# Head-output matmuls and product matmuls in opposite column halves of TensorE, in turns

## The chip, the cores and the metric

The kernel runs on one core of a Trainium2 chip. The metric is the time of one execution on the device in microseconds (us); the median over several runs is given. TensorE multiplies, VectorE (DVE), ScalarE (ACT) and GpSimd (POOL) do the rest, and SyncE (SP) issues most transfers.

## The reference

The input x is 128 batches of 128 rows of 768 numbers, adj 128 matrices of 128 x 128; all is f32. The layer is a pre-norm attention with a mask and a bias from adj, 12 heads of 64.

```python
h = jnp.maximum(_layernorm(x, axis=-1), 0.0)
q = _split_heads(h @ Wq + bq)           # also k and v
scores = jnp.einsum('bhqd,bhkd->bhqk', q, k) / jnp.sqrt(HD)
scores = scores + beta * adj[:, None]
scores = jnp.where(adj[:, None] > 0, scores, -9e15)
probs = jax.nn.softmax(scores, axis=-1)
out = jnp.einsum('bhqk,bhkd->bhqd', probs, v)
return x + out.transpose(0, 2, 1, 3).reshape(B, N, D)
```

## The kernel before

The batches go through in 32 groups of four (G is 0 to 31), so that a group has 512 rows. For each group three slices of the projections are computed: "qk0" (queries and keys of heads 0 to 5), "v" (all values) and "qk1" (queries and keys of heads 6 to 11). Each slice is a 2 x 3 by 3 x 3 block product done with 15 block products in place of 18, on sums of blocks; only the first slice of group 0 is done plainly (L575). The function `slice_of` runs the 15 products in order. `product` (L385) does one: for each of two halves i of its output and each of two halves c of the contraction, it issues two matmuls (L401), one into the lower 64 output partitions (q = 0) and one into the upper 64 (q = 64). Output partitions 0 to 63 and 64 to 127 belong to the two column halves of TensorE, so each matmul uses 64 of its 128 columns. Both matmuls of a pair read the same moving operand of 256 columns, with different weights. Each f32 matmul stands in the trace as two records (two passes), each with its own load of 64 weight columns.

A product adds into a PSUM bank of its chain (a, b, c or d, the third entry of `PRODUCTS`); after the product, DVE (L427 for q and k, L418 and L413 for v) or ACT (L423) reads the bank out, and the next product of the same chain adds on. Eight PSUM banks are handed out in the order in which they were given back (`take`, `give`).

The attention of a group is laid into the slices that follow. `scores` (L437) does the score matmuls (L448) for three pairs of heads at once behind product 1 of a slice, adds the mask and bias on DVE (L452), and takes exponentials on ACT (L455), which gives the tiles e. Behind products 5, 8 and 11 `attend` (L474) puts one generator into the queue `between`. The generator, `attend_steps` (L477), does the head outputs of one pair of heads (i = 0, 1) for the four batches of the group (r and g, two each): in each step one matmul of 65 columns into each column half (L486; 64 columns of v and one of ones that sums the weights). Every turn of the queue, `turn` (L380), runs one step: 

```python
    def turn():
        while between and next(between[0], None) is None:
            between.popleft()
```

`product` calls `turn` four times, behind each pair of its matmuls. An attend has eight steps, so it lies over two products. When the four head outputs of one r are in a bank, `weigh` (L457) divides them by their sums on DVE (L460, L461, L463, L467; in group 0 the division is on ACT, L470), and the bank is given back. At the end GpSimd adds the result to x (L495) and SP stores it (L496). The last group uses other functions for its last heads (`scores_half`, `attend_half`), which the change leaves as they are.

Of the kernel before, what the change touches and what calls it, by code (L numbers as in the profile page):

```python
# [17 lines left out]
P = 128  # L18
# [103 lines left out]
def direct(ctx, tc, x, adj, wq, bq, wk, bk, wv, bv, beta, out, bad):  # L122
# [12 lines left out]
    HD = D // HEADS  # L135
# [244 lines left out]
# [5 lines that stand above are left out]
    def product(G, sl, n, order):  # L385

        an, bn, chain, uses = PRODUCTS[n]
        mine = [i for i in order if PRODUCTS[i][2] == chain]
        first = n == mine[0]
        if first:  # L390
            banks[chain] = take()
        p = banks[chain].rearrange("p (i w) -> p i w", i=2)
        a, b = A[G, an], wt[sl, bn]
        for i in range(2):
            for c in range(2):
                if sl == "v":
                    lhs, rhs = a[:, c, i * N:(i + 1) * N], b[:, c, :]
                else:
                    lhs, rhs = b[:, c, i * P:(i + 1) * P], a[:, c, :]
                for q in range(0, P, HD):  # L400
                    nc.tensor.matmul(p[q:q + HD, i, :], lhs[:, q:q + HD], rhs, start=(first and i == 0 and c == 0),  # L401
                                     stop=(c == 1), skip_group_check=True)
                turn()
        for (r, j), sign in uses:
            key = (G, sl, r, j)
            if sl == "v":
                got = p.rearrange("p g (h d) -> p (g h) d", d=HD)
                if key not in vt:
                    vt[key] = vring[nv[0] % len(vring)]
                    nv[0] += 1  # L410
                    o4 = vt[key].rearrange("p (g h) e -> p g h e", g=2)[:, :, :, 0:HD]
                    bias = bv_b[:, j * 2 * P:(j + 1) * 2 * P].rearrange("p (h d) -> p h d", d=HD)
                    added[G] = nc.vector.tensor_tensor(o4, bias[:, None, :, :].to_broadcast([P, 2, 4, HD]),  # L413
                                                        p.rearrange("p g (h d) -> p g h d", d=HD),
                                                        ALU.add if sign > 0 else ALU.subtract)
                else:
                    o = vt[key][:, :, 0:HD]
                    added[G] = nc.vector.tensor_tensor(o, o, got, ALU.add if sign > 0 else ALU.subtract)  # L418
            elif key not in qk:
                t = qk[key] = work.tile([P, 2, H2], F32, tag="qk", name=f"{sl}_{G}_{r}_{j}", bufs=8)  # L420
                oc = j + 3 * int(sl[2])
                for i in range(2):
                    opened[0] = nc.scalar.activation(t[:, i, :], p[:, i, :], AF.Identity, bias=bqk[:, i, oc:oc + 1],  # L423
                                                     scale=float(sign))
            else:
                t = qk[key]
                added[G] = nc.vector.tensor_tensor(t, t, p, ALU.add if sign > 0 else ALU.subtract)  # L427
        if n == mine[-1]:
            give(banks.pop(chain))
# [27 lines left out]
    def weigh(G, oc, r, pa, o):  # L457

        t = stat.tile([P, 2, 4], F32, tag="sm", name=f"sm_{G}_{oc}_{r}")
        nc.vector.tensor_scalar(t[:, 0], pa[:, :, HD], TINY, None, op0=ALU.max)  # L460
        nc.vector.reciprocal(t[:, 1], t[:, 0])  # L461
        s = seen[:, 8 * r:8 * r + 8]
        nc.vector.tensor_tensor(s, s, t.rearrange("p i b -> p (i b)"), ALU.max)  # L463

        def divide():
            if G:
                nc.vector.tensor_mul(o, pa[:, :, 0:HD], t[:, 1, :, None].to_broadcast([P, 4, HD]))  # L467
            else:
                for b in range(4):
                    nc.scalar.activation(o[:, b], pa[:, b, 0:HD], AF.Copy, scale=t[:, 1, b:b + 1])  # L470

        return divide

    def attend(G, oc):  # L474
        between.append(attend_steps(G, oc))

    def attend_steps(G, oc):  # L477
        o = work.tile([P, 2, 4, HD], F32, tag="o", name=f"o_{G}_{oc}", bufs=2)
        for r in range(2):
            bank = take()  # L480
            pa = bank[:, 0:4 * VE].rearrange("p (b e) -> p b e", e=VE)
            for g in range(2):
                for i in range(2):
                    h = 2 * oc + i
                    for q in range(0, P, HD):
                        nc.tensor.matmul(pa[q:q + HD, 2 * g + i, :], es[G, oc, i][:, 2 * r + g, q:q + HD],  # L486
                                         vt[G, "v", r, h // 4][:, 4 * g + h % 4, :], start=True, stop=True,
                                         skip_group_check=True)
                    if g == i == 1:
                        weigh(G, oc, r, pa, o[:, r])()  # L490
                        give(bank)
                    if r + g + i < 3:
                        yield True
        t = xo[G, oc]
        nc.gpsimd.tensor_add(t, t, o.rearrange("p a (b j) d -> p (a b) (j d)", j=2))  # L495
        nc.sync.dma_start(out[G * GRP:(G + 1) * GRP, :, oc * P:(oc + 1) * P].rearrange("g n d -> n g d"), t)  # L496
        yield True
# [58 lines left out]
    def slice_of(G, sl, todo, order=range(len(PRODUCTS))):  # L556
        for at, n in enumerate(order):
            product(G, sl, n, order)
            for f in todo.get(at, ()):
                f()  # L560
# [372 lines left out]
```

## Time and profile before

| what | value |
|---|---|
| median of 4 runs (lowest to highest) | 2882.28 us (2881.76 to 2882.48) |
| the profiled execution | 2882.06 us |
| its span, first to last instruction | 2880.2 us |
| granted TensorE clock | 0.999 of full |
| busy PE / weight loads / DVE / ACT / POOL | 100% / 70% / 69% / 28% / 12% |
| L401 matmul records | 22800, 256 columns |
| L486 matmul records | 6048, 65 columns |
| L448 matmul records | 6048, 128 columns |

The page of the profile has the busy time of each engine, the granted clock by slices of the span, the chain of work that ended last (followed back from the last instruction), and groups of instructions by line, with busy time, mean duration of one, and the idle time of the engine before them. PE is TensorE's matmuls, PEld its weight loads. The durations of matmul records are modelled and overlap; times from start to start tell what one costs.

### The profile page before, as it was taken

How to read it: one execution, taken by the hardware profiler on the slowest of the kernel's cores; microseconds unless marked ns; L12 is line 12 of the kernel's file. 1: busy time of each engine (PE TensorE's matmuls, PEld its weight loads, DVE VectorE, ACT ScalarE, POOL GpSimd, SP SyncE). 2: the span in 40 equal slices, each digit the busy share in tenths (PEclk: the TensorE clock that was granted, in tenths of full speed). 3: DMA queues.
4: the chain of work that ended last, by engine and by line, in shares of the span. 5: the costliest groups of instructions: out<-in, count | busy, mean ns of one | idle time of the engine just before them, and what ended most of it. 6: DMA issues, size and time to landing. Idle time of an engine off the chain costs nothing.

```text
span 2880.2 us, 81474 instructions
## 1 busy us (share of the span) xinstructions
PE 2871.2 (100%) x35330; PEld 2010.6 (70%) x35330; DVE 1974.2 (69%) x4503; ACT 814.1 (28%) x1750; POOL 334.8 (12%) x320
## 2 busy tenths in 40 slices
PE   9999999999999999999999999999999999999999
PEld 7766667666676666766667766677666676666766
DVE  7867666676666676766766667667676676766665
ACT  2522222232331323313232232322222222323221
POOL 3111011110111110110101101011010111101100
PEclk9999999999999999999999999999999999999999
DMA  9222223222232222332222322223222232222311
GB/s 203 77 61 77 64 79 84 80 68 65 78 88 82 67 70 68 88 87 63 77 70 81 86 66 78 64 82 84 69 79 63 79 84 79 69 69 73 88 38 42
DMA packets 418907, 220.93 MB, mean 77 GB/s; under 512 B 110704, under 2 KB 418160, under 8 KB 418544
## 3 DMA queue, kind: packets, MB, share of 16 engines
q1 hardware_dynamic: 412864, 213.45, 27.2%
q8 instruction: 277, 4.54, 0.7%
q0 software_dynamic: 3808, 1.84, 0.5%
q10 hardware_dynamic: 1872, 0.40, 0.1%
q14 instruction: 86, 0.70, 0.1%
HBM read 164.76 MB, written 50.33 MB: 75 GB/s over the span
## 4 chain that ended last, share of the span: by engine, by line
PE 99%; DVE 0%; DMA 0%; issue 0%; SPq 0%; DVEq 0%
PE bank L401 86%; PE bank L448 6%; PE bank L486 6%; PE bank L575 1%; DMA x<-in_x_dram 0%; PE bank L511 0%; PE bank L529 0%; PE bank L626 0%; DVE o L467 0%; DVE strow L607 0%; DVE e L515 0%; SPq L169 0%; PE bank L278 0%; DVE rows L621 0%; DVE xo L538 0%
## 5 line engine op out<-in xcount | busy, mean ns | idle before, releaser
L401 PE MATMUL bank<-S,qk_T 128*64 128x256 f32 x7056 | 867.5, 380 | 0.0
L427 DVE TENSOR_TENSOR qk<-qk,bank 128x512 f32<-128x512 f32 x630 | 425.5, 676 | 394.3 <-PE bank L401 391.0
L423 ACT ACTIVATE qk<-bank,bqk 128x256 f32<-128x256 f32 x756 | 316.5, 470 | 1133.8 <-PE bank L401 947.1
L486 PEld LDWEIGHTS bank<-v,e 128*64 128x64 f32 x6048 | 433.2, 137 | 220.4
L401 PEld LDWEIGHTS bank<-S,qk_T 128*64 128x64 f32 x7056 | 454.7, 137 | 173.3 <-ACT e L455 5.0
L401 PE MATMUL bank<-S,qk_B 128*64 128x256 f32 x4032 | 543.4, 380 | 0.0
L495 POOL TENSOR_TENSOR xo<-xo,o 128x512 f32<-128x512 f32 x189 | 252.5, 1336 | 2258.6 <-DVE o L467 1587.3
L401 PE MATMUL bank<-A,qk_T 128*64 128x256 f32 x4032 | 490.1, 379 | 0.0
L486 PE MATMUL bank<-v,e 128*64 128x65 f32 x6048 | 430.8, 221 | 0.0
L401 PE MATMUL bank<-v_T,S 128*64 128x256 f32 x3584 | 421.8, 380 | 0.0
L455 ACT ACTIVATE e<-e 128x512 f32<-128x512 f32 x378 | 227.7, 629 | 655.3 <-DVE e L452 654.8
L418 DVE TENSOR_TENSOR v<-v,bank 128x512 f32<-128x512 f32 x320 | 220.0, 687 | 232.4 <-PE bank L401 230.6
L401 PEld LDWEIGHTS bank<-v_T,S 128*64 128x64 f32 x3584 | 254.8, 137 | 130.4 <-issue 5.7
L401 PEld LDWEIGHTS bank<-A,qk_T 128*64 128x64 f32 x4032 | 262.8, 137 | 100.8 <-issue 0.2
L452 DVE SCALAR_TENSOR_TENSOR e<-bank,biasT 128x512 f32<-128x512 f32 x378 | 231.9, 683 | 85.4 <-PE bank L448 85.4
L401 PEld LDWEIGHTS bank<-S,qk_B 128*64 128x64 f32 x4032 | 236.3, 138 | 55.6 <-issue 0.2
L401 PE MATMUL bank<-v_B,S 128*64 128x256 f32 x2048 | 243.2, 379 | 0.0
L401 PE MATMUL bank<-v_T,A 128*64 128x256 f32 x2048 | 237.9, 379 | 0.0
L331 ACT ACTIVATE x<-x,block 128x192 f32<-128x192 f32 x464 | 217.6, 536 | 65.7 <-DMA block<-row 63.7
L338 DVE STREAM_TRANSPOSE A<-x 128x256 f32<-128x256 f32 x378 | 213.2, 612 | 4.0 <-ACT x L331 4.0
L401 PEld LDWEIGHTS bank<-v_B,S 128*64 128x64 f32 x2048 | 147.3, 137 | 73.8
L401 PEld LDWEIGHTS bank<-v_T,A 128*64 128x64 f32 x2048 | 147.1, 137 | 73.9
(93 smaller groups left out, 1668.8 us busy)
## 6 DMA issues: line engine op xcount, KB each, us to landing
x<-in_x_dram SPq DMA_DIRECT2D x504, 96.0 KB, 2.7
xo<-in_x_dram SPq DMA_DIRECT2D x189, 256.0 KB, 3.1
out_dram<-xo SPq DMA_DIRECT2D x189, 256.0 KB, 2.4
half<-in_x_dram SPq DMA_DIRECT2D x232, 192.0 KB, 2.5
adj<-in_adj_dram SPq DMA_DIRECT2D x128, 64.0 KB, 2.7
block<-row SPq DMA_DIRECT2D x464, 1.0 KB, 1.7
qk_T<-in_L_gnn_Wq_dram SPq DMA_DIRECT2D x13, 128.0 KB, 4.1
qk_T<-in_L_gnn_Wk_dram SPq DMA_DIRECT2D x13, 128.0 KB, 3.8
```

The costliest lines, as they stand in the source:

```text
L331: nc.scalar.activation(t, t, AF.Relu, bias=shift[G, n], scale=rstd[G, n])
L338: last = nc.vector.transpose(t[:, :, g * N:(g + 1) * N].rearrange("p c (b i) -> p c b i", i=SQ), src)
L401: nc.tensor.matmul(p[q:q + HD, i, :], lhs[:, q:q + HD], rhs, start=(first and i == 0 and c == 0), stop=(c == 1), skip_group_check=True)
L418: added[G] = nc.vector.tensor_tensor(o, o, got, ALU.add if sign > 0 else ALU.subtract)
L423: opened[0] = nc.scalar.activation(t[:, i, :], p[:, i, :], AF.Identity, bias=bqk[:, i, oc:oc + 1], scale=float(sign))
L427: added[G] = nc.vector.tensor_tensor(t, t, p, ALU.add if sign > 0 else ALU.subtract)
L448: nc.tensor.matmul(ps[oc, i][k:k + HD, g * N:(g + 1) * N], t[r, 1, at][:, k:k + HD], t[r, 0, at], start=True, stop=True)
L452: taken[0] = nc.vector.scalar_tensor_tensor(e, ps[oc, i].rearrange("p (g n) -> p g n", g=GRP), SCORE_CAP * ISCALE, biasT[G], op0=ALU.min, ...
L455: nc.scalar.activation(e, e, AF.Exp, scale=1.0 / ISCALE)
L486: nc.tensor.matmul(pa[q:q + HD, 2 * g + i, :], es[G, oc, i][:, 2 * r + g, q:q + HD], vt[G, "v", r, h // 4][:, 4 * g + h % 4, :], start=Tru ...
L495: nc.gpsimd.tensor_add(t, t, o.rearrange("p a (b j) d -> p (a b) (j d)", j=2))
L575: last = nc.tensor.matmul(p[:, i, at], b[:, c, i * P:(i + 1) * P], a[:, c, at], start=(k == 0 and i == 0 and c == 0), stop=(c == 1), skip_ ...
```

## The change

A step of `attend_steps` becomes two matmuls into the same column half (heads i = 0 and 1), first the upper half (q = 64), then the lower. `turn` is called behind each single matmul of a product and no longer behind a pair: behind the product's matmul into the lower half comes a step into the upper half, and the other way round. A product has eight turns now, and an attend, still of eight steps, lies in one product.

```diff
@@ product
                 for q in range(0, P, HD):
                     nc.tensor.matmul(p[q:q + HD, i, :], lhs[:, q:q + HD], rhs, start=(first and i == 0 and c == 0),
                                      stop=(c == 1), skip_group_check=True)
-                turn()
+                    turn()
@@ attend_steps
             for g in range(2):
-                for i in range(2):
-                    h = 2 * oc + i
-                    for q in range(0, P, HD):
+                for q in (HD, 0):
+                    for i in range(2):
+                        h = 2 * oc + i
                         nc.tensor.matmul(pa[q:q + HD, 2 * g + i, :], es[G, oc, i][:, 2 * r + g, q:q + HD],
                                          vt[G, "v", r, h // 4][:, 4 * g + h % 4, :], start=True, stop=True,
                                          skip_group_check=True)
-                    if g == i == 1:
+                    if g == 1 and q == 0:
                         weigh(G, oc, r, pa, o[:, r])()
                         give(bank)
-                    if r + g + i < 3:
+                    if not (r == g == 1 and q == 0):
                         yield True
```

The order of the matmuls on TensorE, as logical matmuls (P a product's, E a head output's; 0 and 64 the column half):

```
before:  P0 P64 E0 E64   P0 P64 E0 E64   ...   eight times, over two products
after:   P0 E64 E64 P64 E0 E0   ...            four times, in one product
```

## The prediction

> **What bounds the kernel now.** I read the page first: busy shares, clock, chain, groups. Then, in one stretch where a head-output step runs (1006 to 1012 us), the chain in order of time, and last the timeline cut so narrowly that single records can be counted.
>
> ```profile
> span 2880.2 us, 81474 instructions
> PE 2871.2 (100%) x35330; PEld 2010.6 (70%) x35330; DVE 1974.2 (69%) x4503; ACT 814.1 (28%) x1750; POOL 334.8 (12%) x320
> PEclk9999999999999999999999999999999999999999
> PE 99%; DVE 0%; DMA 0%; issue 0%; SPq 0%; DVEq 0%
> PE bank L401 86%; PE bank L448 6%; PE bank L486 6%; PE bank L575 1%; DMA x<-in_x_dram 0%; PE bank L511 0%; PE bank L529 0%; PE bank L626 0%; DVE o L467 0%; DVE strow L607 0%; DVE e L515 0%; SPq L169 0%; PE bank L278 0%; DVE rows L621 0%; DVE xo L538 0%
> L486 PE MATMUL bank<-v,e 128*64 128x65 f32 x6048 | 430.8, 221 | 0.0
> L460 DVE TENSOR_SCALAR sm<-bank 128x4 f32<-128x4 f32 x384 | 59.5, 155 | 68.8 <-PE bank L486 68.8
> ```
>
> The chain that ended last is 99% TensorE at full granted clock. 86% are product matmuls (L401, call one P), 6% head-output matmuls (L486, call one E). No engine holds TensorE up, so only what TensorE itself spends can be saved, 6% at the very most.
>
> ```profile
> 1006.89 0.12 PE bank L486 x4
> 1007.00 0.43 PE bank L401 x4
> 1007.43 0.12 PE bank L486 x4
> 1007.55 0.43 PE bank L401 x4
> ```
>
> Each piece has four records: one matmul into each column half, and each f32 matmul makes two passes, each with its own weight load (22800 records of L401 are 1425 products of 8 matmuls). So a pair of P costs 0.43 us, a pair of E 0.12 us.
>
> Are the halves already working side by side? The timeline from 1006.28 to 1006.30 gives the first line below; that from 1006.495 to 1006.505 the second.
>
> ```profile
> 1006.28 0.39 PE L401 MATMUL bank<-S,qk_B 128*64 128x256 f32 x2
> 1006.28 0.59 PE L401 MATMUL bank<-S,qk_B 128*64 128x256 f32 x3
> ```
>
> Two records start within 0.02 us (in the trace, 6 ns apart), the third 0.22 us later. One half cannot start two passes of 216 ns within 6 ns, so the first two are the first passes of both halves. Yet in the program the first half's second pass stands ahead of the second half's first. So each half keeps its own queue, and a pass of one half overtakes an earlier instruction of the other. Both halves are busy all the time already.
>
> **The cost of a matmul in one half**, as means over all starts in the trace: P pass to P pass 216.28 ns; E pass to E pass 56.67; last E pass to P 58.33; the first P pass behind an E 217.29; last P pass to E 215.83. From the first two, a column costs (216.28 - 56.67)/(256 - 65) = 0.836 ns and a pass 2.35 ns beside. A pair of P is 432.6 ns; P and E together 548.1, so E adds 115.6, of which 2 x 65 x 0.836 = 108.6 is columns.
>
> **The change, part by part.** No instruction is added or removed on any engine, no shape changes. What moves:
>
> (1) Order on TensorE. Before: P0 P64 E0 E64, eight times, over two products. After: P0, two E into the upper half, P64, two E into the lower, four times, in one product; the next product has no E. Each half then runs P, E, E: 432.6 + 2 x 115.6 = 663.8 ns in steps that fall 231 ns apart. An attend has 8 P and 8 E in each half: before 8 x 548.1 = 4385 ns; after 4 x 663.8 + 4 x 432.6 = 4386 ns. Equal: the work of each half is the same and neither was idle, so an E beside a P of the other half only displaces the P that was there.
>
> (2) The edges between E and P. One E costs 1.66 (58.33 for 56.67) + 1.01 (217.29 for 216.28) - 0.45 (215.83 for 216.28) = 2.2 ns in switching. After, two E share one switch. 189 attends x 8 = 1512 pairs; half of 1512 x 2.2 = 3.3 us is 1.7 us of gain. Bounds: all 3.3 us saved, if a load beside a foreign matmul is free; 3.3 us lost, if an E behind an E pays the same switch and a step out of line pays another. I take -1.7, the value that the rows give directly.
>
> (3) Waits moved. The turn now stands behind each half's matmul, so E's first load, which waits for e, v and a bank, has one P (P64) queued behind it that stood ahead of it. Cover: e's exponentials end 4.3 us or more before the first E in every attend of the trace, the bank is the one longest free, v was finished a slice earlier. Cost nothing; without that cover TensorE would stand still for the rest of the wait.
>
> (4) VectorE. The four operations of weigh (155 + 169 + 160 + 417 = 0.90 us, L460 to L467) for the second bank come one product earlier, ahead of that product's own readout. Behind them in VectorE's queue stands the readout of the bank of that product's chain; chain c is written again three products later. In the trace its slack from readout to rewriting is 3.0 us in the median (products 6 to 9 and 9 to 12). It loses 0.90 and the 0.46 us (4 x 115.6 ns) that the following product gets shorter: 1.6 us remain. Only the first group has less (0.22 us): one stall of 1.36 - 0.22 = 1.1 us, in the range, not in the sum.
>
> (5) GpSimd's add (L495) and SP's store (L496) are issued up to one product earlier, behind the same predecessors; GpSimd is 12% busy, SP's queue moves with it. Nobody on the chain waits for either.
>
> Sum against the profiled execution: 2882.06 us = span 2880.2 + 1.9 around it. Span after 2878.5. The median of the runs is 0.2 above that execution, so 2882.28 - 1.7 = 2880.6 us.
>
> [...]
>
> **Rivals.**
>
> A, likeliest: the halves are independent, as summed. Own range 2878 to 2887 (3.3 us either way, and 1.1).
>
> B, slower: the halves are independent only while in step. Place: the second P of each step. Every pair in the trace runs 6 ns apart, both halves streaming the same moving operand; never has one half run a different operand, or run two whole matmuls ahead. After the change the upper half would be two E (four passes) ahead of an unfinished P. If P64 can't start until P0 is done (an order of completion, or a shared read of the operand), a step costs 2 x 432.6 = 865 ns in place of 664: 4 x 189 x 0.201 = 152 us, time 3034 us. It decides if run-ahead reaches less than two matmuls. Against it: in the scores (L448) four tiles run so, each with its two passes queued, and the overtaking is there already by one pass in every pair. For it: nothing in the trace shows it further.
>
> C, slightly slower: VectorE's lumps. If its other work in that stretch (transposes, row statistics) takes more than the 1.6 us of slack left, the next product of chain c waits. Price: 63 slices with attends x up to 0.3 us = 19 us, time up to 2901. Against it: median lags of the readouts are 0.9 to 2.4 us, with slack besides.
>
> D, faster: what a pass costs beside its columns hides behind the other half's long pass. All of it for the E's: 1512 x (115.6 - 108.6) = 10.6 us, time 2871.7. Against it: one matmul's end and the next one's weights are the affair of one half. For it: both halves always switch within 6 ns of each other, so the trace never shows a switch beside a pass in full flow.
>
> **How the numbers follow.** A 0.68, B 0.15, C 0.07, D 0.10. The time is A's: 2880.6. The range takes in A and D, 2870, and C to 2900; left out are B and a little. About 0.2% (5.8 us) is what a measurement of this kernel can tell from no change: A lies within it, D beyond it at 0.10, B and C (mostly) at 0.22.
>
> **What would show it.** Right: in the chain, L401 and L486 keep 86% and 6% (the cut between them may blur, since they now overlap); PE's idle before L401 stays 0.0; in a narrow window, E records start in one half between two starts of P; a step of P and two E repeats every 0.66 us. B: steps repeat every 0.86 us and the span grows by 150 us. C: L401 shows idle time ended by DVE L427. Wrong altogether if PE's pass durations (216 or 57 ns from start to start) change when the halves carry different operands: I have assumed them equal.

## The result, and the profile after

The changed kernel takes 2884.93 us (median of 40 runs, 2884.22 to 2886.56) against 2882.25 us before (60 runs): a ratio of 1.0011, 95% interval 1.0006 to 1.0015. It is 2.7 us slower; the forecast was 1.7 us faster. The profiled execution took 2884.51 us, its span 2882.7, 2.5 more than before. The 40 times stand at two levels, 26 from 2884.2 to 2885.2 and 14 from 2885.8 to 2886.6.

Four lines of the page after: the span, the chain by line, the one group of product matmuls that shows idle time, and the head-output matmuls (L488 now).

```profile
span 2882.7 us, 81472 instructions
PE bank L401 83%; PE bank L488 8%; PE bank L448 6%; PE bank L577 1%; DVE A L338 0%; DMA x<-in_x_dram 0%; DVE e L452 0%; PE bank L513 0%; PE bank L531 0%; PE bank L628 0%; DVE S L344 0%; ACT o L470 0%; DVE qk_T L226 0%; DVE qk L427 0%; DVE o L467 0%
L401 PE MATMUL bank<-S,qk_B 128*64 128x256 f32 x4032 | 593.8, 380 | 2.1 <-ACT qk L423 2.1
L488 PE MATMUL bank<-v,e 128*64 128x65 f32 x6048 | 509.2, 221 | 0.0
```

The chain is still almost wholly TensorE. The second to fourth lines differ from before in two ways: the cut between L401 and L488 has moved (86% and 6% before, by the same line), since the two now overlap, and there is 2.1 us of idle time that was not there, ended by ScalarE's readout of a bank (L423). The chain's line also names ScalarE now (L470), which it did not before. The prediction had named 0.0 of idle time before L401 as a sign of being right.

Where the span grew is found by subtracting the two executions product by product (start of each product's first matmul). The difference is -0.05 us up to product 8 of slice qk1 of group 0 (but for starts that only the new place of the head outputs shifts), +2.27 us at product 9, 2.32 at the end of that slice and 2.43 at the end of the span. So nearly all of it is one place. The timeline of TensorE there, and of ScalarE, in the kernel after:

```profile
87.13 1.90 PE L401 MATMUL bank<-A,qk_T 128*64 128x256 f32 x16
91.17 0.43 PE L401 MATMUL bank<-S,qk_B 128*64 128x256 f32 x1 [2.15 <-ACT qk L423]
85.11 1.94 ACT L423 ACTIVATE qk<-bank,bqk 128x256 f32<-128x256 f32 x5 [3.46 <-DVE qk L427]
88.83 1.93 ACT L470 ACTIVATE o<-bank,sm 128x64 f32<-128x64 f32 x8 [1.78 <-DVE sm L461]
90.63 0.49 ACT L423 ACTIVATE qk<-bank,bqk 128x256 f32<-128x256 f32 x1
```

The same stretch of ScalarE before:

```profile
85.11 2.30 ACT L423 ACTIVATE qk<-bank,bqk 128x256 f32<-128x256 f32 x6 [3.41 <-DVE qk L427]
89.48 0.93 ACT L470 ACTIVATE o<-bank,sm 128x64 f32<-128x64 f32 x4 [2.07 <-DVE sm L461]
90.57 0.93 ACT L470 ACTIVATE o<-bank,sm 128x64 f32<-128x64 f32 x4 [0.16 <-DVE sm L461]
```

Product 6 opens a tile of q and k, so its bank (chain c) is read out by two activations of ScalarE. Before, both ran in a row of six readouts, ahead of all divisions. After, the row has five; the sixth stands behind eight divisions (L470), which exist on ScalarE in group 0 alone and now belong to one product. The divisions wait for VectorE (`sm`), and product 9, which writes the same bank again, waits for the sixth readout: 2.15 us of idle TensorE.

### The profile page after: what moved, and what is told of

It reads as the page before. It is cut to its first block, busy times and chain, and to the rows that moved or that the text cites. A ratio compares the mean times of both kernels' runs of the same rounds, so it can differ in the third digit from the quotient of the medians.

```text
span 2882.7 us, 81472 instructions
## 1 busy us (share of the span) xinstructions
PE 2871.2 (100%) x35330; PEld 2078.4 (72%) x35330; DVE 2000.1 (69%) x4503; ACT 806.0 (28%) x1750; POOL 335.1 (12%) x320
## 3 DMA queue, kind: packets, MB, share of 16 engines
q0 software_dynamic: 3808, 1.84, 0.5%
## 4 chain that ended last, share of the span: by engine, by line
PE 99%; DVE 1%; DMA 0%; ACT 0%; issue 0%; SPq 0%; DVEq 0%; ACTq 0%
PE bank L401 83%; PE bank L488 8%; PE bank L448 6%; PE bank L577 1%; DVE A L338 0%; DMA x<-in_x_dram 0%; DVE e L452 0%; PE bank L513 0%; PE bank L531 0%; PE bank L628 0%; DVE S L344 0%; ACT o L470 0%; DVE qk_T L226 0%; DVE qk L427 0%; DVE o L467 0%
## 5 line engine op out<-in xcount | busy, mean ns | idle before, releaser
L401 PE MATMUL bank<-S,qk_T 128*64 128x256 f32 x7056 | 824.1, 380 | 0.0
L401 PEld LDWEIGHTS bank<-S,qk_T 128*64 128x64 f32 x7056 | 500.4, 137 | 237.7 <-ACT e L455 5.0
L423 ACT ACTIVATE qk<-bank,bqk 128x256 f32<-128x256 f32 x756 | 316.5, 470 | 1152.1 <-PE bank L401 965.4
L401 PE MATMUL bank<-S,qk_B 128*64 128x256 f32 x4032 | 593.8, 380 | 2.1 <-ACT qk L423 2.1
L401 PE MATMUL bank<-A,qk_T 128*64 128x256 f32 x4032 | 526.6, 379 | 0.0
L488 PE MATMUL bank<-v,e 128*64 128x65 f32 x6048 | 509.2, 221 | 0.0
L488 PEld LDWEIGHTS bank<-v,e 128*64 128x64 f32 x6048 | 471.6, 137 | 42.1
L401 PE MATMUL bank<-v_T,S 128*64 128x256 f32 x3584 | 421.8, 380 | 0.0
L401 PEld LDWEIGHTS bank<-S,qk_B 128*64 128x64 f32 x4032 | 347.1, 137 | 85.5 <-ACT qk L423 2.6
L401 PEld LDWEIGHTS bank<-A,qk_T 128*64 128x64 f32 x4032 | 319.3, 137 | 119.1 <-issue 0.2
L401 PEld LDWEIGHTS bank<-v_T,S 128*64 128x64 f32 x3584 | 254.8, 137 | 130.4 <-issue 5.7
L401 PE MATMUL bank<-v_B,S 128*64 128x256 f32 x2048 | 243.2, 379 | 0.0
L401 PE MATMUL bank<-v_T,A 128*64 128x256 f32 x2048 | 237.9, 379 | 0.0
L413 DVE TENSOR_TENSOR v<-bv_b,bank 128x512 f32<-128x512 f32 x192 | 131.9, 687 | 107.4 <-PE bank L401 107.4
L401 PEld LDWEIGHTS bank<-v_B,S 128*64 128x64 f32 x2048 | 147.2, 137 | 73.9
```

## The experiments

Two theories were set against each other. **S**: the whole loss is this stall. **T**: it is spread over all 189 attends, 14 ns each. Whether ScalarE or VectorE is at fault was asked besides.

**Group 0 as before, the rest changed.** `turn` gets the half q, and an attend of group 0 uses the old steps and is only advanced behind pairs.

```diff
-        between.append(attend_steps(G, oc))
+        between.append((G > 0, (attend_steps if G > 0 else pair_steps)(G, oc)))
...
-        while between and next(between[0], None) is None:
+        while between and (q or between[0][0]) and next(between[0][1], None) is None:
```

> The change for groups 1 to 31, the old order (pairs, two products per attend) for group 0. Theory S (one stall in group 0: ScalarE's second half of the readout of product 6 stands behind eight divisions): the stall is gone, TensorE shows no idle time ended by ACT, and the time is before + 0.1 to 0.4 us, 2882.4 to 2882.7. Rival T (the loss is spread over all attends, in switches between matmuls or VectorE's lumps, 2.7 us / 189 = 14 ns each): 183 of 189 attends keep it, 2884.8.

Measured: 2882.53 us (11 runs), before 2882.19 in the same series; 1.0001, interval 0.9991 to 1.0010. No idle time of TensorE is ended by L423. The highest of these runs (2882.59) lies below the lowest of the changed kernel (2884.22), and product by product, groups 1 to 31 lose 0.1 us together. T is out.

**Only group 0 changed**: the same code with `G == 0`.

> The reverse: only group 0 (six attends) in the new order, all other groups as before. Theory S: the whole loss is here, 2884.5 to 2885, with one idle stretch of about 2.1 us on TensorE at product 9 of qk1 of group 0. Rival T: 6 of 189 attends, 2882.3. If the two levels of the changed kernel's times (2884.8 and 2886.3) come from this stall, they show here too.

Measured: 2884.88 us (11 runs, as in the two that follow); 1.0011, interval 1.0002 to 1.0020. TensorE's idle time ended by L423 is there again, 2.1 us. Six attends of 189 bring the whole loss. Eight runs lie from 2884.3 to 2885.0, three from 2886.5 to 2886.6: the two levels are here too. The experiment before has one level (2882.1 to 2882.6), and so have the two that follow.

**The second weigh of group 0 one turn later**, so that four of the eight divisions go behind the readout.

```diff
                     if g == 1 and q == 0:
+                        if G == 0 and r == 1:
+                            yield True
                         weigh(G, oc, r, pa, o[:, r])()
```

> The change, but in group 0 the second weigh (and its four divisions) is issued one turn later, behind the product's readout. On ScalarE the second half of the readout of product 6 then stands behind four divisions instead of eight. Theory S: it ends 0.93 us earlier (four divisions took 0.93 us), so the stall shrinks from 2.15 to about 1.2 us and the time is 2883.9 to 2884.1. Rival V (the stall comes from VectorE's work ahead of the divisions alone): no change, 2884.9.

Measured: 2883.72 us, a little under the time expected; 1.0005, interval 0.9996 to 1.0014. ScalarE and TensorE in this kernel's timeline:

```profile
89.55 0.93 ACT L470 ACTIVATE o<-bank,sm 128x64 f32<-128x64 f32 x4 [1.77 <-DVE sm L461]
90.34 0.49 ACT L423 ACTIVATE qk<-bank,bqk 128x256 f32<-128x256 f32 x1
90.89 0.43 PE L401 MATMUL bank<-S,qk_B 128*64 128x256 f32 x1 [1.10 <-ACT qk L423]
```

The stall went from 2.15 to 1.10 us, a little more than the 0.93 us of four divisions. So the divisions ahead of the readout set it.

**The divisions of group 0 on VectorE**, as in the other groups (`if G:` to `if True:` in `divide`).

> The change, with the divisions of group 0 on VectorE as in all other groups (12 of 0.42 us in place of 48 of 0.32 us on ScalarE). Theory S: ScalarE's readout of product 6 has nothing ahead of it, the stall of 2.15 us at product 9 is gone, 2882.4 to 2882.8, unless VectorE, which has weight sums in this stretch, is late itself: then a stall shows that ends on DVE L427. Rival V: stall unchanged or longer, 2884.9 or more.

Measured: 2882.42 us; 1.0001, interval 0.9992 to 1.0010. ScalarE's six readouts stand in one row again, and product 9 starts without idle time:

```profile
85.62 2.29 ACT L423 ACTIVATE qk<-bank,bqk 128x256 f32<-128x256 f32 x6 [3.45 <-DVE qk L427]
89.38 0.38 PE L401 MATMUL bank<-S,qk_B 128*64 128x256 f32 x1
```

VectorE, with more work there, is in time. This is the changed kernel without its fault, and it is not faster than before.

**How far may a half run ahead?** The prediction's rival B hung on that, and no trace showed it. In the first kernel a step goes into the half whose product matmul it follows (`for q in (0, HD)`, and the end of a step at q = HD): P0 E0 E0 P64 E64 E64.

> The change, but each step goes into the half whose product matmul it follows (P0 E0 E0 P64 E64 E64), in all groups. This asks how far one half may run ahead: the upper half's P now stands behind three whole matmuls of the lower half (12 instructions with their weight loads). Independent queues that hold 8 or more waiting instructions a half: no loss beside the changed kernel's, 2884 to 2886. Queues of 4: each step of 664 ns becomes 1094, 4 x 189 x 0.43 = 325 us more, 3210. Queues of 6: 978, 238 us more, 3123. Rival B of the prediction (in step only): lower and upper half one after the other, 1327 a step, 501 us more, 3386.

Measured: 3130.16 us; 1.0860, interval 1.0842 to 1.0878. TensorE's timeline in one attend:

```profile
1008.12 0.22 PE L488 MATMUL bank<-v,e 128*64 128x65 f32 x1
1008.12 0.43 PE L401 MATMUL bank<-A,qk_T 128*64 128x256 f32 x1
1008.17 0.34 PE L488 MATMUL bank<-v,e 128*64 128x65 f32 x3
1008.39 0.38 PE L401 MATMUL bank<-A,qk_T 128*64 128x256 f32 x1
1008.61 0.22 PE L488 MATMUL bank<-v,e 128*64 128x65 f32 x1
1008.61 0.43 PE L401 MATMUL bank<-A,qk_T 128*64 128x256 f32 x1
```

From 1008.12 to 1008.61 there are two passes of P (1008.12 and 1008.39) and four of E: half a step in 0.489 us, where the changed order needs 0.332. The halves overlap only in part. A whole step lasts 0.978 us, the 978 ns of one case of the expectation; the queue that the expectation puts behind this figure was the author's assumption, and no run shows it. In the second kernel, made from the kernel before, a product issues four matmuls into one half and then four into the other:

```diff
-        for i in range(2):
-            for c in range(2):
+        for q in range(0, P, HD):
+            for i, c in ((0, 0), (0, 1), (1, 0), (1, 1)):
...
-                turn()
+        for _ in range(4):
+            turn()
```

> The kernel before, with the order inside each product changed: four matmuls into the lower half, then four into the upper (16 instructions in a row for one half), and the head-output pairs of the four turns behind the product. Independent queues of 8 or more a half, or one long window: a product stays 1.73 us, 2882 to 2890. Queues of 6: 1.84 us a product, 1425 x 0.11 = 162 us more, 3044. Queues of 4: 2.28 us, 780 us more, 3660. In step only: 3.46 us, 5350.

Measured: 3341.64 us; 1.1593, interval 1.1574 to 1.1613. Products without head outputs last 1.840 us from start to start in the median (1.727 before), the 1.84 of the same case in this expectation. That is 161 us over 1425 products. The other 298 us, which the expectation had left out, lie around the other matmuls: about 240 in the products that carry head-output pairs and those next behind them, about 50 at the score matmuls. TensorE's timeline where the upper half's four matmuls of one product (v_B) are followed by the lower half's of the next (v_T):

```profile
1006.61 0.43 PE L400 MATMUL bank<-v_T,S 128*64 128x256 f32 x1
1006.82 0.38 PE L400 MATMUL bank<-v_B,S 128*64 128x256 f32 x1
1006.87 0.38 PE L400 MATMUL bank<-v_T,S 128*64 128x256 f32 x1
1007.03 0.38 PE L400 MATMUL bank<-v_B,S 128*64 128x256 f32 x1
1007.09 0.38 PE L400 MATMUL bank<-v_T,S 128*64 128x256 f32 x1
1007.25 0.38 PE L400 MATMUL bank<-v_B,S 128*64 128x256 f32 x1
```

In both timelines the first pass of the other half begins when three passes of the running half have yet to begin: here v_B at 1006.82, 1007.03 and 1007.25, in the first kernel three of E behind 1008.12. In most places of both traces it begins 5 to 7 ns behind the running half's pass ahead of those three. The two step times add up from the passes: the first pass of a run takes 266 ns, the others 216, so that half a step is 266 + 216 + 6 = 488 ns in the first kernel and half a product 266 + 3 x 216 + 6 = 920 ns in the second. What makes the other half wait until then, no run shows.

**What the second level is.** Stalls were made on purpose in the kernel before: the readout of product 6 in qk1 of groups 1 to 30 repeats its first half.

```diff
+                again = (9, 11, 12, 13, 15)[G % 5] if sl == "qk1" and n == 6 and 0 < G < NG - 1 else 0
-                for i in range(2):
+                for i in [0] * again + [0, 1]:
```

> The kernel before, with stalls made on purpose: in qk1 of groups 1 to 30 the readout of product 6 is preceded by 9, 11, 12, 13 or 15 repeats of its first half on ScalarE (by G modulo 5), so that product 9 waits about 0.7, 1.5, 1.9, 2.3 or 3.2 us, six times each; 58 us in sum, 2940. It asks for the second level of the changed kernel's times, 1.5 us above the first in a third of the executions. Theory H (an idle of over about 2 us sometimes makes the clock drop to half for a while): stretches of clock 0.5 show in the record of the granted clock behind the longer stalls and none behind those of 0.7 and 1.5, and each costs about 1.5 us more. Rival N (nothing to do with the clock): the clock stays at 1.0 throughout, and the time is the sum of the stalls.

Measured: 2930.23 us; 1.0166, interval 1.0146 to 1.0187. The idle stretches were at most 1.4 us (1.6 by the count used below), shorter than meant, and the clock stayed at 1.0 (0.999 in the mean, as before). This leaves the question open; longer stalls followed.

> As the stalls on purpose, with 17, 20, 23, 26 or 30 repeats: the stalls of 9 to 15 repeats cost only 0.9 to 1.6 us, too short to speak on the question. Now 2 to 7 us of idle are expected. Theory H (an idle of over about 2 us sometimes makes the clock drop to half): stretches of clock 0.5 in the record behind the longer ones, each costing 1 to 2 us beside the idle itself. Rival N: the clock stays at 1.0.

Measured: 2985.41 us; 1.0356, interval 1.0326 to 1.0386. From start to start the 30 stalls are 1.9 to 2.6 us (not 2 to 7), and behind ten of them the record of the granted clock has a stretch of 3.4 us at 0.5; its mean over the span is 0.994. Two of the stalls in the table by stretches (time, PE, PEld, DVE, ACT, POOL busy with counts, the granted clock, DMA), each with the stretch behind it:

```profile
277.10:279.20 2.10, 0.16 (x3) 0.03 (x2) 0.20 (x2) 1.93 (x5) 1.26 (x1) 1.00 0.40 119
280.50:283.90 3.40, 3.40 (x18) 2.26 (x15) 2.28 (x5) 0.00 (x0) 0.00 (x0) 0.50 0.36 105
647.30:649.20 1.90, 0.06 (x3) 0.04 (x2) 0.16 (x2) 1.74 (x4) 0.28 (x1) 1.00 0.65 199
650.50:653.90 3.40, 3.40 (x32) 2.05 (x28) 2.75 (x5) 0.00 (x0) 0.00 (x0) 1.00 0.37 108
```

The clock column is 0.50 behind the first stall and 1.00 behind the second; the same 3.4 us hold 18 matmul passes in the one case and 32 in the other. The length of the stall alone does not decide: of six stalls with 2.33 to 2.34 us of idle (a pass counted as 216 ns), four were followed by the half clock and two were not. What decides beside the length, no run shows. Between groups of equal repeats a halving cost 1.2 to 1.6 us.

The changed kernel was run twice more for a profile at its second level.

> The changed kernel as it is, for a profile of an execution at the second level of its times (2886.3, 14 of 40 executions). Theory H: at that level the record of the granted clock has a stretch of 0.5 behind the stall at 88.9 to 91.2 us, worth 1.5 us; at the first level (2884.8) none. Rival N: the clock is 1.0 at both levels, and the 1.5 us stand elsewhere, in a longer stall.

> The changed kernel once more, since one look in three falls on the second level of its times: the same expectations, a clock of 0.5 behind the stall by theory H, a longer stall at full clock by rival N.

Measured: 2884.87 and 2884.53 us, both at the first level, with the clock at 1.0 behind the stall. So no trace shows the second level. Its cause is argued: the stall is 2.5 us from start to start, 2.3 us idle by the count above, about as long as the six made stalls of which four were followed by the half clock, and the 1.2 to 1.6 us of a halving match the 1.5 us between the levels. The half clock came behind ten of the 30 made stalls; 14 of 40 and 3 of 11 executions were at the second level. The four traces of this stall (three of the changed kernel, one of the change in group 0 alone) are all at the first level. That the second level comes with this stall is shown by the first four experiments, with one exception: one of the three executions of the kernel before in the last series took 2883.79 us, some 1.5 above the others, and it has no trace.

## Why the prediction was wrong

The sign was wrong; the range and "within 0.2%" held. Two steps failed: part (2), a saving that did not come, and part (4), which looked for the cost of the moved weigh in the wrong engine's queue. Of the 4.3 us between forecast (2880.6) and result, 4.1 are found in these two; the rest is what one execution differs from the medians.

**Rival A's frame held.** One step in the kernel after:

```profile
1009.97 0.38 PE L401 MATMUL bank<-S,qk_B 128*64 128x256 f32 x1
1009.98 0.40 PE L488 MATMUL bank<-v,e 128*64 128x65 f32 x4
1010.18 0.40 PE L401 MATMUL bank<-S,qk_B 128*64 128x256 f32 x2
1010.40 0.22 PE L488 MATMUL bank<-v,e 128*64 128x65 f32 x1
1010.42 0.38 PE L401 MATMUL bank<-S,qk_B 128*64 128x256 f32 x1
1010.46 0.34 PE L488 MATMUL bank<-v,e 128*64 128x65 f32 x3
1010.63 0.38 PE L401 MATMUL bank<-S,qk_B 128*64 128x256 f32 x1
```

Four passes of P and eight of E begin in 0.66 us, as forecast. The halves are independent in this order, and a step of P, E, E takes 664.9 ns in the trace after (means of the pass to pass times in one half), where 663.8 were summed.

**Part (2), the edges: wrong, worth 1.8 us of the miss.** One switch was to be saved for every second E. In the trace after, the passes of two E in a row take 56.7, 58.3, 60.8 and 56.0 ns: 231.8 for two, 115.9 each, where a pair added 115.6 before. The change from one E to the next takes the 58.3 ns that the change from an E to a P took before, and the second E's first pass takes 60.8; why, no run shows. A product that carries an attend and a plain one take 2659.3 + 1727 = 4386.3 ns against 2 x 2192.5 = 4385.0. By these means the 189 attends lose 0.2 us, by the subtraction of the two executions 0.1; 1.7 were to be gained.

**Part (4), the moved weigh: wrong, worth 2.3 us.** It was priced on VectorE's queue, by 0.90 us of its operations. The stall came on ScalarE's queue, which the part did not go through: in group 0 the four divisions of a weigh are there, 0.93 us each time, and they also wait for VectorE. The part did find that group 0 had the least room, but at another product (12, 0.22 us of slack), with 1.1 us, and it left that out of the sum as a bound. No stall came there. Product 9 of group 0 had 1.5 us of slack. The order of ScalarE's queue after the change, the readout's second half behind eight divisions, belongs to the program and not to the run, so it could have been read beforehand.

**Part (3)** held: no load of an E waits for e, v or its bank. **Part (5)** held: nobody on the chain waits for GpSimd.

**The rivals.** B did not come: a step took 0.66 us, not 0.86. What B feared is real in part all the same: the order P0 E0 E0 P64 E64 E64 costs 248 us more than the kernel before, though not the 501 put on halves that run one after the other. C came near: work in a lump ahead of a bank's readout, but on ScalarE, and once instead of in every slice. D did not show: two E cost 231.8 ns and not the 217 of their columns.

## What to carry to other kernels

When both halves of TensorE are busy all the time, pairing a short matmul with a long one gained nothing here: count the busy time of each half first. When a step is moved, go through the queue of every engine that it issues on, in every variant of the step (here one group of 32 divides elsewhere), and ask which bank readout is now behind it. Interleave column halves finely: here runs of three matmuls in one half cost 248 us, and runs of four 459.

## What the runs showed of the hardware

- In the changed order matmuls of 256 and of 65 columns ran in the two column halves at once: an E began 0.01 us behind the first pass of the P ahead of it and before that P's second pass, and a step lasted 664.9 ns, 663.8 by the work of one half. With runs of three matmuls in one half the same step lasted 978 ns; with runs of four a product lasted 1840 ns for 1727.
- Behind ten of 30 made stalls of 1.9 to 2.6 us from start to start, TensorE's granted clock was 0.5 for 3.4 us; behind 30 made stalls with at most 1.4 us of idle by the profile it stayed at 1.0.
- A stall of 2.3 us idle (a pass counted as 216 ns) came with two levels of time from run to run, 2884.8 and 2886.3 us; that the clock makes the second is argued.
